# A two-layer perceiver: the state space cut into a leading part and a recurrence, and experts built in single banks with one gelu each

## The chip, the cores and the metric

The kernel runs on one core of a Trainium2 chip. The time is device microseconds of one execution. Before the change three runs gave 2102.15, 2106.83 and 2114.19 us, a median of 2106.83 us. A further execution was taken with the hardware profiler; it took 2099.58 us.

## The reference

`x` holds 64 sequences of 32 tokens with 256 features, 2048 tokens in all. Six residual steps follow each other, three per layer:

```python
x = x + _L0_xattn_ref(_layernorm(x), ctx, ctx, mask, ...)   # cross-attention
x = x + _L0_attn_ref(_layernorm(x), ...)                    # RWKV time and channel mix
x = x + _L0_ffn_ref(_layernorm(x), Wg, We, be)              # 8 experts 256->256, top 2
x = x + _L1_xattn_ref(_layernorm(x), ctx, ...)              # 16 heads, quantised linears
x = x + _L1_attn_ref(_layernorm(x), ...)                    # state space, 16 states
x = x + _L1_ffn_ref(_layernorm(x), ...)                     # 8 experts 256->512->256
```

The change touches the last two. The state space projects to 512 channels `x_main` and 512 channels `z`, runs a causal convolution of width 4 and a SiLU, and then a recurrence for each channel and each of 16 states, before it multiplies by `silu(z)`, projects back and normalises:

```python
dA = jnp.exp(A[None] * dt[:, :, None])
dBx = dt[:, :, None] * B_t[:, None, :] * x_t[:, :, None]
h = dA * h + dBx
y = jnp.einsum('bdn,bn->bd', h, C_t) + D * x_t
```

The last step computes all eight experts for every token, adds them up and scales the sum by a gate near one:

```python
h = jax.nn.gelu(jnp.einsum('nd,edh->neh', xf, w1) + b1, approximate=False)
y = jnp.einsum('neh,ehd->ned', h, w2) + b2
out = (y * norm_g[:, None, None]).sum(axis=1)
```

## The kernel before

The 2048 tokens are cut into four blocks of 512 (`NBLK`, `BT`), each four tiles of 128 tokens; `x` stays in on-chip memory all through. Each residual step is a stage, and each stage a function that is called once per block: `s0` and `s1` (attention and RWKV of the first layer), `s2` (top-2 experts, matmuls at L625), `s3` (second attention, 16 small tiles per block in `tile3`: scores at L811, exponentials at L813), `s4` (state space, `_stage4`) and `s5` (eight experts, `_stage5`). All matmuls that the change touches are in f32.

*What sets the order.* `layers` emits the stages block by block. The emission order gives each instruction its rank; from it a scheduler makes one fixed order for each engine when the kernel is built, and each engine works its own queue in that order. So an instruction that waits holds up all that stands behind it on its engine. Buffers come from pools: a `tag` with `bufs=n` has n buffers that are used in turn, and a new tile waits until the last reader of the tile that held its buffer is done. The accumulation memory is shared in the second half of the kernel by the bank (128x512 f32): two for `k.ps` (attention), two for `k.psh` (all of the state space, one bank a tile), two for `k.psu` (one tile of two banks: all of `s5` apart from its sums) and two for `k.psacc` (the sums of the experts).

*Emission around the change* (end of `layers`): `s2(1)`, `s3(1)`, `s4(0)`, `s2(2)`, `s2(3)`, and then for b = 1, 2, 3: `s3(b+1)` while there is one, `s4(b)`, `s5(b-1)`; at the end `s5(3)`. Below, "attention b", "recurrence b" and "experts b" are these stages for block b.

*State space, one block.* Statistics and norm, transposes, `project(0..3)` (L929), convolution on DVE, SiLU on ACT, a projection to the rows of B and C (L951), which go to DRAM, and to dt (L959), whose softplus is built of several ACT and DVE steps. GpSimd (POOL) forms `dtx` (L975). Then comes the recurrence: for each of 16 states a load that spreads a row of B and one of C over all partitions (`bc`), and for each pair of channel groups: `g = dtx*B` on POOL (L987, 128x1024), and for each of the two groups an exponential on ACT (L991), a scan on DVE (L992) and a product with C on DVE (L993); then POOL adds `hc` to `y` (L994). Sixteen sequences of 32 lie in one scan of 512; a large dt at each first token makes the decay there vanish. After the last state: `z` (`project(4..7)`), its SiLU and product, the residual's norm, the out-projection (L1004, L1005), and a layer norm whose last steps are on POOL.

*Experts, one block.* Norm and transposes, the gate (L1074 to L1100), and then 16 steps `h` over pairs of hidden chunks of 128. `up(h)` fills two banks: for each chunk one bf16 matmul of three rows, which adds the bias as the sum of three bf16 pieces (L1116), and two f32 matmuls with `w1` (L1118); one gelu of 128x1024 moves both to `hid` (L1120). `down(h)` adds four matmuls with `w2` (L1127) to the sums. `up(h+2)` is emitted ahead of `down(h)`. Then the sums are transposed back, scaled, added to `x` and stored tile by tile (L1144).

Of the kernel before, what the change touches and what calls it, by code (L numbers as in the profile page):

```python
# [8 lines left out]
F32 = mybir.dt.float32  # L9
# [6 lines left out]
P = 128  # L16
# [860 lines left out]
def _stage4(k, w, wk):  # L877

    nc, i = k.nc, k.i
# [29 lines left out]

    def tmp(shape, name):
        return wk.tile(shape, F32, name=name, tag="t4", bufs=3)

    def block(b):
        xs = [k.x[b][:, j, :] for j in range(4)]
        mv, rstd = _stats(k, xs, "4")
        xn = []
        for j in range(4):
            t = wk.tile([P, D], F32, name="xn4", tag="xn4", bufs=4)  # L920
            _norm(k, t, xs[j], mv, rstd, j)
            xn.append(t)
        xT = wk.tile([P, 2, BT], F32, name="xT4", tag="xT4")
        _to_channels(k, xn, lambda c, ps: nc.scalar.copy(xT[:, c, :], ps), ph)

        def project(o):
            ps = ph([P, BT], "inps")
            for c in range(2):
                nc.tensor.matmul(ps, win[:, c, o * P : (o + 1) * P], xT[:, c, :], start=c == 0, stop=c == 1)  # L929
            return ps  # L930

        xc = wk.tile([P, C, 16, T], F32, name="xc", tag="xc", bufs=1)
        for c in range(C):
            xpad = xpads[c % 2]
            nc.scalar.activation(
                xpad[:, :, 3:], project(c).rearrange("p (b t) -> p b t", t=T), AF.Identity, bias=_chan(k, "L1_attn_in_proj_b", c)
            )
            nc.vector.tensor_scalar(
                xc[:, c], xpad[:, :, 0:T], _chan(k, "conv_w0", c), _chan(k, "L1_attn_conv_b", c), ALU.mult, ALU.add
            )  # L940
            for j in range(1, 4):
                nc.vector.scalar_tensor_tensor(
                    xc[:, c], xpad[:, :, j : j + T], _chan(k, f"conv_w{j}", c), xc[:, c], ALU.mult, ALU.add
                )
        nc.scalar.activation(xc, xc, AF.Silu)
        xcf = xc.rearrange("p c b t -> p c (b t)")


        ssm_ps = ph([2 * N, BT], "ssm_ps")
        for c in range(C):  # L950
            nc.tensor.matmul(ssm_ps, wx[:, c, 0 : 2 * N], xcf[:, c, :], start=c == 0, stop=c == C - 1)  # L951
        ssm = tmp([2 * N, BT], "ssm")
        nc.scalar.activation(ssm, ssm_ps, AF.Identity, bias=bx)
        rows = k.dram.tile([2 * N, BT], F32, name="rows", tag="rows", bufs=2)
        nc.sync.dma_start(rows, ssm)

        dt_ps = ph([P, BT], "dt_ps")
        for c in range(C):
            nc.tensor.matmul(dt_ps, wdt[:, c, :], xcf[:, c, :], start=c == 0, stop=c == C - 1)  # L959


        dt = wk.tile([P, BT], F32, name="dt", tag="dt")
# [10 lines left out]
        nc.vector.scalar_tensor_tensor(dt, dt, 0.0, l_, ALU.max, ALU.add)  # L973
        dtx = wk.tile([P, C, BT], F32, name="dtx", tag="dtx", bufs=1)
        nc.gpsimd.tensor_tensor(dtx, xcf, dt.unsqueeze(1).to_broadcast([P, C, BT]), ALU.mult)  # L975

        nc.gpsimd.memset(dt.rearrange("p (b t) -> p b t", t=T)[:, :, 0:1], 1e20)
        y = xcf
        for c in range(C):
            nc.scalar.activation(y[:, c, :], y[:, c, :], AF.Copy, scale=_chan(k, "L1_attn_D", c))  # L980
        bc_rows = rows.rearrange("(two n) t -> n two t", two=2)
        for n in range(N):
            bc = wk.tile([P, 2, BT], F32, name="bc", tag="bc", bufs=2)
            nc.sync.dma_start(bc, bc_rows[n].partition_broadcast(P))
            for c2 in range(0, C, 2):
                g = wk.tile([P, 2, BT], F32, name="g", tag="g", bufs=3)
                nc.gpsimd.tensor_tensor(g, dtx[:, c2 : c2 + 2], bc[:, 0:1, :].to_broadcast([P, 2, BT]), ALU.mult)  # L987
                hc = wk.tile([P, 2, BT], F32, name="hc", tag="hc", bufs=2)
                for c in range(2):
                    h = ph([P, BT], "h")  # L990
                    nc.scalar.activation(h, dt, AF.Exp, scale=A[:, c2 + c, n : n + 1])  # L991
                    nc.vector.tensor_tensor_scan(h, h, g[:, c, :], 0.0, ALU.mult, ALU.add)  # L992
                    nc.vector.tensor_tensor(hc[:, c, :], h, bc[:, 1, :], ALU.mult)  # L993
                nc.gpsimd.tensor_tensor(y[:, c2 : c2 + 2], y[:, c2 : c2 + 2], hc, ALU.add)  # L994

        for c in range(C):
            zs = tmp([P, BT], "zs")
            nc.scalar.activation(zs, project(C + c), AF.Silu, bias=_chan(k, "L1_attn_in_proj_b", C + c))
            nc.gpsimd.tensor_tensor(y[:, c], y[:, c], zs, ALU.mult)
        for j in range(4):  # L1000
            _norm(k, xn[j], xs[j], mv, rstd, j)
# [12 lines left out]
    return block  # L1014
# [5 lines left out]
def _stage5(k, w, tmp, out):  # L1020
# [17 lines left out]

    at = CHAN_AT["L1_ffn_b1"]
    left = tmp.tile([P, E * H], F32, name="left", tag="left")  # L1040
    nc.vector.tensor_copy(left, k.chan[:, at : at + E * H])
    b1d = k.dram.tile([3, E * H, P], BF16, name="b1d", tag="b1d")
    for q in range(3):
        piece = tmp.tile([P, E * H], BF16, name="piece", tag=f"piece{q}")
        nc.vector.tensor_copy(piece, left)
        nc.vector.tensor_tensor(left, left, piece, ALU.subtract)
        pc_ps = k.ps.tile([E * H, P], BF16, name="pc_ps", tag="s")
        nc.tensor.transpose(pc_ps, piece, k.identb)
        rows = tmp.tile([E * H, P], BF16, name="pc_rows", tag=f"pc_rows{q}")
        nc.scalar.copy(rows, pc_ps)  # L1050
        nc.scalar.dma_start(b1d[q], rows)
    one3 = w.tile([3, 1], BF16, name="one3", tag="one3")
    nc.gpsimd.memset(one3, 1.0)
# [6 lines left out]
    def block(b):  # L1060
        xs = [k.x[b][:, j, :] for j in range(4)]
        mv, rstd = _stats(k, xs, "5")
        xn = []
        for j in range(4):
            t = k.wk5.tile([P, D], F32, name="xn5", tag="xn5", bufs=4)
            _norm(k, t, xs[j], mv, rstd, j)
            xn.append(t)
        xT = k.wk5.tile([P, 2, BT], F32, name="xT5", tag="xT5", bufs=1)
        _to_channels(k, xn, lambda c, ps: nc.scalar.copy(xT[:, c, :], ps), ps)
# [33 lines left out]
        w1, w2, b1 = {}, {}, {}  # L1103

        def up(h):
            e, q = divmod(h, H)
            if q == 0:
                w1[e] = k.wk5.tile([P, 2, H * P], F32, name="w1", tag="w1")
                w2[e] = k.wk5.tile([P, H, D], F32, name="w2", tag="w2")
                b1[e] = k.wk5.tile([3, H, P], BF16, name="b1e", tag="b1e")  # L1110
                nc.sync.dma_start(w1[e], w1d[e])
                nc.sync.dma_start(w2[e], w2d[e])
                nc.sync.dma_start(b1[e], b1d[:, H * e : H * e + H, :])
            u = ps([P, 2, BT], "up")
            for f in range(2):
                nc.tensor.matmul(u[:, f, :], b1[e][:, q + f, :], one3.to_broadcast([3, BT]), start=True, stop=False)  # L1116
                for c in range(2):
                    nc.tensor.matmul(u[:, f, :], w1[e][:, c, (q + f) * P : (q + f + 1) * P], xT[:, c, :], start=False, stop=c == 1)  # L1118
            t = k.wk5.tile([P, 2, BT], F32, name="hid", tag="hid")
            nc.scalar.activation(t, u, AF.Gelu)  # L1120
            return t

        def down(h, t):
            e, q = divmod(h, H)
            for f in range(2):
                for o in range(2):
                    nc.tensor.matmul(  # L1127
                        acc[o], w2[e][:, q + f, o * P : (o + 1) * P], t[:, f, :], start=h + f == 0, stop=h + f == E * H - 1
                    )

        t = up(0)
        for h in range(0, E * H, 2):
            later = up(h + 2) if h + 2 < E * H else None
            down(h, t)
            t = later
        res = k.wk5.tile([P, 2, BT], F32, name="res", tag="hid")
        for o in range(2):
            nc.scalar.activation(res[:, o, :], acc[o], AF.Identity, bias=b2s[:, o : o + 1])
        for j in range(4):
            rT = ps([P, D], "rT")  # L1140
            for o in range(2):
                nc.tensor.transpose(rT[:, o * P : (o + 1) * P], res[:, o, j * P : (j + 1) * P], k.ident)  # L1142
            t = k.wk5.tile([P, D], F32, name="o5", tag="xn5", bufs=4)
            nc.vector.scalar_tensor_tensor(t, rT, gt[:, j : j + 1], xs[j], ALU.mult, ALU.add)  # L1144
            nc.sync.dma_start(out[(4 * b + j) * P : (4 * b + j + 1) * P, :], t)
# [4 lines left out]
def layers(k, out):  # L1150
# [32 lines left out]
    with right, left:  # L1183
        pool = opened(left, "left")
        k.psh, k.psu, w4 = pool("psh", 2, **psum), pool("psu", 1, **psum), pool("w4", 1)
        s4 = _stage4(k, w4, pool("wk4", 2))
        with right2:
            s2(1)
            s3(1)
            s4(0)  # L1190
            s2(2)
            s2(3)
        k.psacc, w5 = pool("psacc", 2, **psum), pool("w5", 1)
        with ExitStack() as es:
            s5 = _stage5(k, w5, opened(es, "right")("tmp5", 1), out)
        k.wk5 = pool("wk5", 2)
        for b in range(1, NBLK):
            if b + 1 < NBLK:
                s3(b + 1)
            s4(b)  # L1200
            s5(b - 1)
# [82 lines left out]
```

## Time and profile before

| | |
|---|---|
| median of three runs | 2106.83 us (2102.15 to 2114.19) |
| profiled execution | 2099.58 us |
| its span | 2097.8 us |
| mean granted TensorE clock | 0.838 of full speed |
| instructions | 20886 |
| ACT table loads at the gelu's line / at the exponential's L991 | 47 / 33, 1283 ns each |

The span is the time between the first and the last instruction in the trace. In a group's row, the columns are line, engine, operation, output and inputs, shape and count, then busy us and mean ns of one, then idle us of the engine just before these instructions and what ended most of that idle time. The engines are PE (matmul), PEld (weight load, beside PE), DVE, ACT, POOL and SP (which only issues loads and stores here). One f32 matmul with 512 columns leaves two matmul records in the trace. The 40 slices of the page show the granted clock in tenths; it swings between half and full within the span:

```profile
PE   4778967668989878885879999979999859873798
...
PEclk8677977878989977555887999978999969986799
```

Stages by first and last instruction of their lines in the trace, in us from the span's start:

| stage | from | to |
|---|---|---|
| attention 1 | 755 | 1017 |
| recurrence 0 (POOL, L975 to L994) | 799 | 998 |
| attention 2, with experts 0 | 1110 | 1410 |
| recurrence 1 | 1126 | 1323 |
| attention 3, with experts 1 | 1411 | 1700 |
| recurrence 2 | 1469 | 1645 |
| recurrence 3, with experts 2 | 1752 | 1912 |
| out-projection of block 3 (PE) | 1912 | 1933 |
| experts 3 (PE) | 1950 | 2095 |

### The profile page before, as it was taken

Reading aid. Unit: us, or ns where it says so; the run is one execution under the profiler, and the core shown is the slowest. Engines: PE = TensorE matmul, PEld = TensorE weight load, DVE = VectorE, ACT = ScalarE, POOL = GpSimd, SP = SyncE. Lnnn points to the kernel's source line nnn. Section 1 sums busy time; section 2 is a strip of 40 time slices with the busy share of each in tenths; the row PEclk is TensorE's granted clock in tenths of the full one; section 3 lists DMA queues with packets and bytes.
Section 4 is the critical chain, followed back from the end, with each engine's and each line's share of the span. In section 5 each row is a group of like instructions: output and inputs, shape, how many; then the busy total and the mean of one; then the engine's idle time right before and its main releaser. Section 6 shows DMA issues by size and latency. Waiting matters only on the chain. (4 is left out here: it accounts for less than half of the span.)

```text
span 2097.8 us, 20886 instructions
## 1 busy us (share of the span) xinstructions
PE 1711.6 (82%) x6778; PEld 831.9 (40%) x6778; DVE 1349.9 (64%) x2559; ACT 920.8 (44%) x1932; POOL 1009.7 (48%) x1078
## 2 busy tenths in 40 slices
PE   4778967668989878885879999979999859873798
PEld 2334534334545433442434444434444423322333
DVE  4588493765584567999666888545888663775100
ACT  3445342302434235554115677526777527652111
POOL 4445445312121315888414788430888545996100
PEclk8677977878989977555887999978999969986799
DMA  7654232210000101232002333111233103340011
GB/s 236 222 182 148 92 116 80 72 41 0 21 21 21 58 7 55 61 71 61 0 0 68 105 107 105 31 33 49 71 113 108 41 0 91 101 121 21 30 60 40
DMA packets 88007, 150.10 MB, mean 72 GB/s; under 512 B 8040, under 2 KB 52442, under 8 KB 85850
## 3 DMA queue, kind: packets, MB, share of 16 engines
q1 hardware_dynamic: 85188, 147.79, 23.0%
q10 hardware_dynamic: 2710, 0.98, 0.2%
q8 instruction: 53, 0.87, 0.2%
q14 instruction: 56, 0.46, 0.1%
HBM read 137.81 MB, written 10.94 MB: 71 GB/s over the span
## 5 line engine op out<-in xcount | busy, mean ns | idle before, releaser
L992 DVE TENSOR_TENSOR_SCAN h<-h,g 128x512 f32<-128x512 f32 x256 | 305.9, 1218 | 57.9 <-ACT h L991 45.3
L987 POOL TENSOR_TENSOR g<-dtx,bc 128x1024 f32<-128x1024 f32 x128 | 299.1, 2352 | 73.5 <-DMA bc<-rows 51.6
L994 POOL TENSOR_TENSOR xc<-xc,hc 128x1024 f32<-128x1024 f32 x128 | 300.0, 2351 | 48.0 <-DVE hc L993 32.3
L1118 PE MATMUL up<-xT,w 128*128 128x512 f32 x512 | 279.0, 654 | 0.0
L1127 PE MATMUL acc<-hid,w 128*128 128x512 f32 x512 | 246.6, 611 | 0.8 <-ACT hid L1120 0.8
L991 ACT ACTIVATE h<-dt,A 128x512 f32<-128x512 f32 x256 | 173.5, 688 | 121.7 <-DVE hc L993 120.4
L811 PE MATMUL sc<-kT,qm 32*128 32x257 f32 x512 | 177.5, 498 | 16.0 <-ACT p L813 10.9
L993 DVE TENSOR_TENSOR hc<-h,bc 128x512 f32<-128x512 f32 x256 | 171.0, 679 | 8.8 <-POOL xc L994 4.9
L813 ACT ACTIVATE p<-sc,nm 128x257 f32<-128x257 f32 x256 | 119.6, 470 | 107.9 <-DVE nm L812 106.8
L812 DVE TENSOR_REDUCE nm<-sc 128x1 f32<-128x257 f32 x256 | 102.6, 416 | 90.8 <-PE sc L811 89.7
L625 PE MATMUL weps<-we,xT 128*128 128x512 f32 x256 | 137.2, 677 | 27.2 <-DVE x L627 26.1
L89 POOL TENSOR_TENSOR rs_t<-rs_r 128x4 f32<-128x4 f32 (+3 forms) x150 | 32.8, 220 | 239.6 <-DVE rs_r L87 204.3
L1127 PEld LDWEIGHTS acc<-hid,w 128*128 128x128 f32 x512 | 93.4, 193 | 104.4 <-issue 102.5
L811 PEld LDWEIGHTS sc<-kT,qm 32*128 32x128 f32 x512 | 79.2, 213 | 125.5 <-ACT p L813 51.3
L1118 PEld LDWEIGHTS up<-xT,w 128*128 128x128 f32 x512 | 87.0, 198 | 94.6 <-issue 93.5
L1120 ACT ACTIVATE hid<-up 128x1024 f32<-128x1024 f32 x64 | 65.5, 1023 | 104.5 <-PE up L1118 103.9
L230 POOL TENSOR_TENSOR cT<-cT,scb 128x2056 f32<-128x2056 f32 x16 | 74.6, 4662 | 52.5 <-DMA scb<-scales 43.0
L929 PE MATMUL inps<-xT,w_L_attn_in_projT 128*128 128x512 f32 x128 | 72.8, 704 | 31.3 <-DVE hc L993 31.3
L525 POOL TENSOR_TENSOR kk<-kk 128x512 f32<-128x512 f32 x32 | 33.2, 1040 | 119.4 <-ACT kk L524 119.4
L1144 DVE SCALAR_TENSOR_TENSOR o<-rT,gt,x 128x256 f32<-128x256 f32 x16 | 7.6, 476 | 128.6 <-PE rT L1142 128.4
L824 PE MATMUL pt_ps<-ident,p 128*128 128x128 f32 x512 | 86.4, 312 | 2.1 <-DVE kT L789 0.8
L625 PEld LDWEIGHTS weps<-we,xT 128*128 128x128 f32 x256 | 50.9, 213 | 88.6 <-issue 59.8
(391 smaller groups left out, 3210.3 us busy)
## 6 DMA issues: line engine op xcount, KB each, us to landing
bc<-rows SPq DMA_DIRECT2D x64, 512.0 KB
w<-in_L_ffn_w_dram SPq DMA_DIRECT2D x64, 512.0 KB
cT<-in_ctxT_dram SPq DMA_DIRECT2D x16, 1028.0 KB
cq<-cq SPq DMA_DIRECT2D x32, 514.0 KB
cn<-in_ctx_dram SPq DMA_DIRECT2D x64, 256.0 KB
scb<-scales SPq DMA_DIRECT2D x16, 514.0 KB
kb<-steps SPq DMA_DIRECT2D x16, 514.0 KB
x<-in_x_dram SPq DMA_DIRECT2D x4, 512.0 KB
```

Source lines behind the costliest of these rows:

```text
L625: nc.tensor.matmul(ps, xT[:, c, r], we[:, c, e : e + 2, :], start=c == 0, stop=c == 1)
L811: nc.tensor.matmul(sc, qm[r, e].rearrange("p l n g -> p (l n g)"), kT[r, :], start=True, stop=True)
L812: nc.vector.tensor_reduce(nm[:, h : h + 1], sc, AX.X, ALU.max, negate=True)
L813: nc.scalar.activation(p[:, h, :], sc, AF.Exp, bias=nm[:, h : h + 1], accum_out=sm[:, e, h : h + 1])
L824: nc.tensor.transpose(pt_ps[:, h, :], p[:, h, m * P : (m + 1) * P], k.ident)
L987: nc.gpsimd.tensor_tensor(g, dtx[:, c2 : c2 + 2], bc[:, 0:1, :].to_broadcast([P, 2, BT]), ALU.mult)
L991: nc.scalar.activation(h, dt, AF.Exp, scale=A[:, c2 + c, n : n + 1])
L992: nc.vector.tensor_tensor_scan(h, h, g[:, c, :], 0.0, ALU.mult, ALU.add)
L993: nc.vector.tensor_tensor(hc[:, c, :], h, bc[:, 1, :], ALU.mult)
L994: nc.gpsimd.tensor_tensor(y[:, c2 : c2 + 2], y[:, c2 : c2 + 2], hc, ALU.add)
L1118: nc.tensor.matmul(u[:, f, :], w1[e][:, c, (q + f) * P : (q + f + 1) * P], xT[:, c, :], start=False, stop=c == 1)
L1127: nc.tensor.matmul(acc[o], w2[e][:, q + f, o * P : (o + 1) * P], t[:, f, :], start=h + f == 0, stop=h + f == E * H - 1)
```

## The change

The state space is cut in two functions. `ahead(b)` holds everything up to dt, with an accumulation bank of its own (`psp`); `recur(b, v)` holds the rest. `xc` gets two buffers, `g` two for three; the SiLU of z is built in pairs in the buffers of `g`, and the residual's norm is built again in a buffer of `hc`. `layers` emits `ahead` of the next block in front of the recurrence of the present one, `s2(2)` in front of both. `psu` becomes one bank.

In the experts the bias matmuls and their three bf16 pieces go. Each hidden chunk is built in the one bank of `psu` and moved to `hid` with its bias added, by DVE for even chunks and by ACT for odd ones; after four chunks one gelu works in place over 128x2048. The down-projection of an expert runs one expert behind the up-projection. With the sums in `psacc`, three banks are in use. `xn5` and the output tile share one buffer of two tiles (four buffers of one before), `res` takes the buffer of `xT5`, and a block's output leaves in two stores.

```diff
-    def block(b):
+    def ahead(b):
+        v = Ctx()
...
-        xc = wk.tile([P, C, 16, T], F32, name="xc", tag="xc", bufs=1)
+        xc = wk.tile([P, C, 16, T], F32, name="xc", tag="xc")
...
+        return v
+
+    def recur(b, v):
+        xs = [k.x[b][:, j, :] for j in range(4)]
+        dt, y = v.dt, v.y
...
-                g = wk.tile([P, 2, BT], F32, name="g", tag="g", bufs=3)
+                g = wk.tile([P, 2, BT], F32, name="g", tag="g", bufs=2)
...
-        for c in range(C):
-            zs = tmp([P, BT], "zs")
-            nc.scalar.activation(zs, project(C + c), AF.Silu, bias=_chan(k, "L1_attn_in_proj_b", C + c))
-            nc.gpsimd.tensor_tensor(y[:, c], y[:, c], zs, ALU.mult)
-        for j in range(4):
-            _norm(k, xn[j], xs[j], mv, rstd, j)
+        for c2 in range(0, C, 2):
+            zs = wk.tile([P, 2, BT], F32, name="zs", tag="g", bufs=2)
+            for f in range(2):
+                nc.scalar.activation(
+                    zs[:, f, :], project(v, C + c2 + f, ph), AF.Silu, bias=_chan(k, "L1_attn_in_proj_b", C + c2 + f)
+                )
+            nc.gpsimd.tensor_tensor(y[:, c2 : c2 + 2], y[:, c2 : c2 + 2], zs, ALU.mult)
+        xn = wk.tile([P, 4, D], F32, name="xe4", tag="hc", bufs=2)
...
+        for n in range(E * H + H):
+            e, q = divmod(n, H)
+            if e < E:
...
+                    hid[e] = k.wk5.tile([P, H, BT], F32, name="hid", tag="hid")
+                u = ps([P, BT], "up")
                 for c in range(2):
-                    nc.tensor.matmul(u[:, f, :], w1[e][:, c, (q + f) * P : (q + f + 1) * P], xT[:, c, :], start=False, stop=c == 1)
-            t = k.wk5.tile([P, 2, BT], F32, name="hid", tag="hid")
-            nc.scalar.activation(t, u, AF.Gelu)
-            return t
...
+                    nc.tensor.matmul(u, w1[e][:, c, q * P : (q + 1) * P], xT[:, c, :], start=c == 0, stop=c == 1)
+                b1 = _chan(k, "L1_ffn_b1", n)
+                if q % 2:
+                    nc.scalar.activation(hid[e][:, q, :], u, AF.Identity, bias=b1)
+                else:
+                    nc.vector.tensor_scalar(hid[e][:, q, :], u, b1, None, ALU.add)
+                if q == H - 1:
+                    nc.scalar.activation(hid[e], hid[e], AF.Gelu)
+            e -= 1
+            if e >= 0:
                 for o in range(2):
                     nc.tensor.matmul(
-                        acc[o], w2[e][:, q + f, o * P : (o + 1) * P], t[:, f, :], start=h + f == 0, stop=h + f == E * H - 1
+                        acc[o], w2[e][:, q, o * P : (o + 1) * P], hid[e][:, q, :], start=n == H, stop=n == E * H + H - 1
                     )
...
-        s4 = _stage4(k, w4, pool("wk4", 2))
+        ahead, recur = _stage4(k, w4, pool("wk4", 2))
         with right2:
             s2(1)
+            v = ahead(0)
             s3(1)
-            s4(0)
             s2(2)
+            later = ahead(1)
+            recur(0, v)
             s2(3)
...
         for b in range(1, NBLK):
+            v = later
             if b + 1 < NBLK:
                 s3(b + 1)
-            s4(b)
+                later = ahead(b + 1)
+            recur(b, v)
             s5(b - 1)
         s5(NBLK - 1)
```

## The prediction

> **What bounds the kernel now.** I read the page's table of engines first, then the windows of busy time cut at the borders of the stages (found by the lines' first and last instructions), then the chain that ended last. No engine is full over the span:
>
> ```profile
> span 2097.8 us, 20886 instructions
> ...
> PE 1711.6 (82%) x6778; PEld 831.9 (40%) x6778; DVE 1349.9 (64%) x2559; ACT 920.8 (44%) x1932; POOL 1009.7 (48%) x1078
> ```
>
> The windows (start:end, length; busy us of PE, weight loads, DVE, ACT, POOL with counts; granted PE clock; DMA share; GB/s):
>
> ```profile
> 799.00:998.00 199.00, 147.62 (x637) 77.60 (x638) 180.90 (x280) 96.98 (x235) 159.31 (x80) 0.54 0.21 56
> 998.00:1126.00 128.00, 108.31 (x321) 52.42 (x320) 79.11 (x223) 26.84 (x46) 32.14 (x101) 0.86 0.07 22
> 1126.00:1323.00 197.00, 185.61 (x805) 80.92 (x804) 168.76 (x249) 138.34 (x255) 155.38 (x78) 0.95 0.32 89
> ...
> 1469.00:1645.00 176.00, 172.19 (x774) 76.80 (x773) 149.86 (x228) 128.78 (x237) 147.90 (x64) 0.98 0.32 96
> ...
> 1752.00:1912.00 160.00, 113.03 (x256) 43.11 (x254) 115.02 (x131) 95.76 (x111) 149.16 (x65) 0.88 0.35 99
> ...
> 1950.00:2097.00 147.00, 139.56 (x328) 57.65 (x328) 5.47 (x22) 21.71 (x23) 2.36 (x12) 0.94 0.15 47
> ```
>
> Row 1 is recurrence 0 beside attention 1: DVE is 91% busy and sets the end. Row 2 is the stretch between two recurrences (top-2 experts of blocks 2 and 3, block 1's projection). Rows 3 and 4 are recurrences 1 and 2 beside attention 2 and 3 and, interleaved, the experts of blocks 0 and 1: PE is 94% and 98% busy, so the experts fill PE while DVE and POOL do the recurrence. Row 5 is recurrence 3 with the experts of block 2 under it: POOL 93%. Row 6 is block 3's experts alone. The chain has that tail in a fixed beat of 7.89 us for two hidden chunks:
>
> ```profile
> 2000.39 1.91 PE up L1118 x4
> 2002.62 1.91 PE up L1118 x4
> 2004.53 3.43 PE acc L1127 x8
> 2008.28 1.91 PE up L1118 x4
> ```
>
> The 2000.39 to 2008.28 beat holds 2 x 1.91 + 3.43 = 7.25 us and, as the rest, two bias matmuls and gaps (0.64). So the end is the sum of three attention stages, the gaps between recurrences, recurrence 3 at POOL's pace, and PE alone in the tail.
>
> **The change, part by part.** Baseline is the profiled execution, 2099.58 us: span 2097.8 and 1.8 around it. The median of the three runs, 2106.83, lies 7.25 above it. Where work goes I read from the fixed order of the changed kernel's instructions on each engine; a PE row of the trace is half a matmul there, because these matmuls leave two records each.
>
> *Leading part (statistics, in-projection, convolution, softplus) ahead of another block's recurrence, with its own bank.* Work is the same; its matmuls, evictions, convolution and one store of B and C rows move on PE, ACT, DVE and SP. In SP's order the store of block 1's rows stands behind all sixteen row loads of recurrence 0 and ahead of those of recurrence 1, so nothing queues behind it that could run earlier: 0. Gain: row 2 ends earlier. The top-2 experts of block 2 now mix with the start of attention 1, so between recurrences 0 and 1 only block 3's experts and a projection are left, about 63 us after attention 1's end at 1012; attention 2 and recurrence 1 start at about 1075, against 1110 and 1126: -35 and -51. Later "ahead" parts still wait for their attention stage, which gives their input, and are followed by the recurrence at once: the 51 to 58 us from attention's end to the product dt*x (52 for block 3, 1700 to 1752) stay. So the overlap is real only for blocks 0 and 1.
>
> *Banks.* The leading part's own bank is taken from the experts: they build each up-projection in one bank where it was two side by side; the recurrence keeps two. What that costs is in the experts' terms and in rival C. *g in two buffers instead of three.* POOL makes g, DVE scans and multiplies (0.68 each), POOL adds (2.35). Bounds: 0 where POOL sets the pace (64 x 2.35 = 150 of recurrence 3's 160), and up to 1 us per pair (32 us a recurrence) where DVE must finish two scans before the next g begins. The scan's group says how near g is to being the last to come:
>
> ```profile
> L992 DVE TENSOR_TENSOR_SCAN h<-h,g 128x512 f32<-128x512 f32 x256 | 305.9, 1218 | 57.9 <-ACT h L991 45.3 <-POOL g L987 5.3 <-POOL xc L994 3.5
> L987 POOL TENSOR_TENSOR g<-dtx,bc 128x1024 f32<-128x1024 f32 x128 | 299.1, 2352 | 73.5 <-DMA bc<-rows 51.6 <-DVE h L992 11.6 <-DVE kT L789 2.8
> ```
>
> Of 57.9 us of idle before all 256 scans ACT's exponential ends 45.3 and g only 5.3, so g is mostly there with time to spare; but a scan that has to free a buffer already holds POOL up for 11.6 in all four. I take 5 us a recurrence at most and 0 in the sum.
>
> *Experts.* 128 bias matmul records of 396 ns go (50.7 us of PE, about 12.7 a block). The 64 gelus of 1023 ns become 32 of twice the width, and 128 plain evictions with bias are added, half on DVE, half on ACT: nearest row is the 128x512 ACT exponential, 688 ns, and the DVE product from the same banks, 679 ns. That is 16 x 0.68 = 11 us per block on each. In the tail the beat becomes 7.25; 16 beats save 10, but the first expert has no down-projection to hide its four evictions (about 4 x 0.9), and the last gelu (2.05) and four down steps stand alone: about 123 us against 130.
>
> *A rule against the row, ACT.* The Trainium skill, "ScalarE: Activation LUTs", section "What ACT_TABLE_LOAD costs", puts a load at about 1283 ns and some 1.4 more for the drain. The trace has the 1283 too, 47 loads at the gelu's line and 33 at the exponential's, 102.6 us. By the rule, one gelu per expert would take half the switches and give back some 100 us of ACT. By the rows it gives nothing: ACT is 44% busy, 60% in row 5, and the tail uses one table. I take 0.
>
> *What the order moves, and this decides.* Before, experts 0 ran inside recurrence 1 and experts 1 inside recurrence 2. In the changed order, half of each expert's evictions stand in DVE's queue, spaced one per some eight instructions of a recurrence, and the experts' first norms stand behind recurrence 1's last scans. On PE, 548 matmuls of attention 2 run in one piece without an expert between them; the 156 matmuls of experts 0 come after it, with block 2's projection, ahead of most of attention 3; experts 1 share PE with attention 3's last 340 matmuls, where no recurrence runs; 92 of experts 2's come beside recurrence 3, and 61 are left behind its output projection. Then experts 3's norms wait for experts 2's last output store, since they share one buffer that was four.
>
> Sum: attention 2 beside recurrence 1, as row 1 but with no experts, takes about what attention 1 took (755 to 1017, 262 us): I take 258, to 1333 (before 1410). *Second rule against a row.* "TensorE: Matmul & The Clock Gate", "The HAM clock gate": PE that has no idle gap above some 3.4 us runs at the full clock. Row 1 has PE busy 148 of 199 us and a clock of 0.54. By the rule the clock would be 1.00 as in busier stretches and only DVE's 121 (recurrence) and about 100 (attention) would bound it: 226 us. I take the row's. Then 58 to recurrence 2 at 1391 (before 1469). Experts 0 hold PE to about 1485 (156 matmuls of 0.9 us with the projection). Attention 3 from there: 211 matmuls x 0.33 = 70, output projection 12, the remaining 340 with 62 of the experts about 150: end 1716, against 1700. Recurrence 3 at 1768, +16, for 160 us; its output projection ends at 1949 (before 1933). After that: layer norm wait 9, of which half is hidden, 53 matmuls of experts 2 x 0.9 = 48, their transposes, store and experts 3's norms 24, experts 3 123, end 10: about 207, against 165. Span 2097.8 + 16 + 42 = 2156; 2158 with what lies around it; on the median's footing 2165.
>
> **Rivals.**
> *A (0.66), above: slower*, because experts 0 leave recurrence 1 and a part of experts 2 comes out behind recurrence 3. Range 2130 to 2200.
> *B (0.13): faster.* Attention 3 packs. For it: rows 3 and 4 show PE can be 94 to 98% busy with experts beside attention, and 51 us fewer of bias. It decides if attention 3 ends before 1647: recurrence 3 then ends 70 sooner, and even with 207 behind it the median is 2095 or less; at 1640, 2089. Against it: 300 us of PE work (attention 3, experts 0, part of experts 1) would have to fit into 1391 to 1640.
> *C (0.14): much slower.* Lockstep: an expert's next up-projection waits for its single bank, whose eviction waits in DVE's queue behind scans that wait for g. At 1 us for each of 32 pairs in two recurrences, +60: 2225. Against it: POOL's pace already is 2.35 us per instruction.
> *D (0.07): no change.* The 77 us won by 1333 pay all of what experts 0 push back, and the tail's 42 are met by what is left of it: 2107.
>
> **How the numbers follow.** Likeliest A, 2165. A measurement of this kernel tells about 0.5% from no change, so 2096 to 2117 is "same". Faster is B, 0.13; same is D, 0.07; slower is A and C, 0.80. The range leaves out less than half of B and half of C: 2094 to 2222. A alone: 2130 to 2200.
>
> **What would show it.** Right: attention 2 beside recurrence 1 at a granted clock near 0.5 and DVE near 90%; experts 0's first up-projection after about 1275; recurrence 3's first g at 1750 to 1790; about 48 us of up and down matmuls of block 2 after recurrence 3's last output projection; experts 3's beat 7.25. Wrong: recurrence 3 starting before 1690 (B), a recurrence longer than 190 us with POOL under 80% (C), or the tail behind recurrence 3's output projection at 165 or less.

## The result and the profile after

The changed kernel took 2181.73 us (median of four runs, 2178.64 to 2184.82) against 2110.51 us for the kernel before on the same footing: a ratio of 1.034, 95% interval 1.029 to 1.038. The profiled execution took 2181.74 us, with a span of 2180.0 us. In one of the runs below (two banks shared by the leading part and the experts) two of 20 executions took 3073 and 3669 us, and its ratio leaves them out.

The page of the changed kernel, in its table of engines and four of its groups (columns as before):

```profile
PE 1770.9 (81%) x6647; PEld 881.3 (40%) x6647; DVE 1398.3 (64%) x2616; ACT 894.9 (41%) x1907; POOL 1009.5 (46%) x1069
...
L997 POOL TENSOR_TENSOR g<-dtx,bc 128x1024 f32<-128x1024 f32 x128 | 300.6, 2353 | 108.2 <-DVE h L1002 43.1
...
L1116 PE MATMUL up<-xT,w 128*128 128x512 f32 x512 | 278.4, 660 | 67.9 <-DVE hid L1121 52.1
L1004 POOL TENSOR_TENSOR xc<-xc,hc 128x1024 f32<-128x1024 f32 x128 | 300.9, 2352 | 22.9 <-DVE hc L1003 22.7
...
L811 PE MATMUL sc<-kT,qm 32*128 32x257 f32 x512 | 216.6, 579 | 15.2 <-ACT p L813 13.3
```

The last group before the change:

```profile
L811 PE MATMUL sc<-kT,qm 32*128 32x257 f32 x512 | 177.5, 498 | 16.0 <-ACT p L813 10.9
```

The bias matmuls, 50.7 us of PE, are gone, and yet PE is busy for 59 us longer. The score matmuls of the attention (L811) have not changed, but one takes 579 ns where it took 498: more of the attention runs at half the clock. An eviction is the instruction that moves a finished tile from its bank to on-chip memory. One wait is new, PE's 52.1 us for DVE's evictions, and one has grown: POOL waits 43.1 us for scans before g, where it waited 11.6.

The windows of the changed kernel, cut at its own stages:

```profile
1086.00:1292.00 206.00, 170.75 (x752) 92.19 (x751) 181.70 (x294) 108.75 (x258) 161.25 (x83) 0.55 0.23 65
...
1390.00:1586.00 196.00, 170.85 (x552) 79.68 (x552) 154.76 (x221) 115.74 (x202) 158.50 (x71) 0.76 0.29 81
1586.00:1728.00 142.00, 135.12 (x640) 66.79 (x640) 59.82 (x166) 61.09 (x139) 24.71 (x71) 0.95 0.12 38
...
1780.00:1958.00 178.00, 119.22 (x238) 49.83 (x237) 141.88 (x167) 83.26 (x106) 153.99 (x81) 0.78 0.30 80
...
1978.00:2042.00 64.00, 49.83 (x117) 21.48 (x116) 12.13 (x31) 12.51 (x12) 10.52 (x32) 0.94 0.21 66
```

Row 1 is recurrence 1 beside attention 2: it had experts inside and a clock of 0.95, and now has none and 0.55. Row 2 is recurrence 2, with experts 0 in its first half. Row 3 is what is left of attention 3, with experts 1: PE is 95% busy, and DVE and POOL, freed of the recurrence, stand at 42% and 17%. Row 4 is all but the ends of recurrence 3, which now takes 180 us. Row 5 is new: the rest of experts 2 with nothing to hide under. The chain through it, start and length in us:

```profile
2023.10 1.92 ACT hid L1123
2025.06 7.15 PE acc L1127 x16
2034.87 2.15 DMA out_dram<-o
2038.70 2.14 DMA out_dram<-o
2051.38 3.79 PE up L1116 x4
```

Block 2's experts end and are stored before block 3's first up-projection starts at 2051.38.

Stage by stage, with the prediction's value between the two traces (us; recurrences by `dtx` and the last sum into `y`; by this measure recurrence 2 before the change ends at 1655, not 1645, and takes 186 us, and recurrence 3 ends at 1916, not 1912):

| | before | predicted | after |
|---|---|---|---|
| recurrence 1 starts | 1126 | 1075 | 1086 |
| attention 2 starts | 1110 | 1075 | 1083 |
| attention 2 ends | 1410 | 1333 | 1343 |
| recurrence 2 starts | 1469 | 1391 | 1390 |
| experts 0 leave PE | 1378 | 1485 | 1487 |
| attention 3 ends | 1700 | 1716 | 1728 |
| recurrence 3 starts | 1752 | 1768 | 1775 |
| recurrence 3 takes | 164 | 160 | 180 |
| out-projection of block 3 ends | 1933 | 1949 | 1977 |
| from there to the end | 165 | 207 | 203 |

### The profile page after: what moved, and what is told of

Same layout as the page of the kernel before. It is cut to its first block, busy times and chain, and to the rows that moved or that the text cites. A ratio compares the mean times of both kernels' runs of the same rounds, so it can differ in the third digit from the quotient of the medians.

```text
span 2180.0 us, 20697 instructions
## 1 busy us (share of the span) xinstructions
PE 1770.9 (81%) x6647; PEld 881.3 (40%) x6647; DVE 1398.3 (64%) x2616; ACT 894.9 (41%) x1907; POOL 1009.5 (46%) x1069
## 5 line engine op out<-in xcount | busy, mean ns | idle before, releaser
L997 POOL TENSOR_TENSOR g<-dtx,bc 128x1024 f32<-128x1024 f32 x128 | 300.6, 2353 | 108.2 <-DVE h L1002 43.1
L1116 PE MATMUL up<-xT,w 128*128 128x512 f32 x512 | 278.4, 660 | 67.9 <-DVE hid L1121 52.1
L1127 PE MATMUL acc<-hid,w 128*128 128x512 f32 x512 | 255.0, 624 | 10.8 <-ACT hid L1123 10.8
L811 PE MATMUL sc<-kT,qm 32*128 32x257 f32 x512 | 216.6, 579 | 15.2 <-ACT p L813 13.3
L1116 PEld LDWEIGHTS up<-xT,w 128*128 128x128 f32 x512 | 97.6, 204 | 204.0 <-issue 93.0
L1127 PEld LDWEIGHTS acc<-hid,w 128*128 128x128 f32 x512 | 100.4, 201 | 136.8 <-issue 116.8
L1121 DVE TENSOR_SCALAR hid<-up,chan 128x512 f32<-128x512 f32 x64 | 47.7, 745 | 158.2 <-PE up L1116 158.1
L811 PEld LDWEIGHTS sc<-kT,qm 32*128 32x128 f32 x512 | 97.2, 249 | 128.2 <-ACT p L813 70.8
L625 PE MATMUL weps<-we,xT 128*128 128x512 f32 x256 | 135.0, 657 | 7.0 <-DVE x L627 6.0
L1119 ACT ACTIVATE hid<-up,chan 128x512 f32<-128x512 f32 x64 | 43.8, 684 | 200.7 <-PE up L1116 200.3
L824 PE MATMUL pt_ps<-ident,p 128*128 128x128 f32 x512 | 100.1, 354 | 5.2 <-ACT pl L818 3.1
L824 PEld LDWEIGHTS pt_ps<-ident,p 128*128 128x128 f32 x512 | 82.3, 184 | 23.5 <-DVE kT L789 9.1
```

The costliest lines, as they stand in the source:

```text
L625: nc.tensor.matmul(ps, xT[:, c, r], we[:, c, e : e + 2, :], start=c == 0, stop=c == 1)
L811: nc.tensor.matmul(sc, qm[r, e].rearrange("p l n g -> p (l n g)"), kT[r, :], start=True, stop=True)
L824: nc.tensor.transpose(pt_ps[:, h, :], p[:, h, m * P : (m + 1) * P], k.ident)
L1116: nc.tensor.matmul(u, w1[e][:, c, q * P : (q + 1) * P], xT[:, c, :], start=c == 0, stop=c == 1)
L1127: nc.tensor.matmul(acc[o], w2[e][:, q, o * P : (o + 1) * P], hid[e][:, q, :], start=n == H, stop=n == E * H + H - 1)
```

## The experiments

My theory was that the experts leave the recurrences because with one bank and the last rank they find no place in the order beside the scans. The rivals were the single bank as a price at every chunk, the two g buffers, and the split itself. Each run has its own ratio to the kernel before, with its interval. The kernel before took 2103 to 2111 us beside the different runs, so where times of different runs are set against each other, a few us say nothing, and the ratios are the better guide.

**Experts emitted first.** In the changed kernel:

```diff
-            recur(b, v)
             s5(b - 1)
+            recur(b, v)
```

> The changed kernel with one line moved: the experts of block b-1 are emitted ahead of recurrence b instead of behind it, so that they have the higher rank; banks, buffers, evictions and gelus are those of the change. Theory (the experts are pushed out of the recurrences because, with the lower rank, their evictions stand behind the recurrence's scans in DVE's order): experts 0 run beside attention 2 and recurrence 1 again, nothing of experts 2 is left behind block 3's out-projection, and the early gain of some 35 to 50 us stays: 2060 to 2100 us. Rival 1 (one bank for the up-projection costs PE a wait at each chunk, wherever the experts stand): 2140 us or more. Rival 2 (two g buffers stretch the recurrences): 2150 us or more, recurrence 3 still at 178 us. If the experts' evictions delay the scans as much as they gain, recurrences 1 and 2 grow to 230 us and the time is near 2140.

Measured: 2111.41 us, ratio 1.003 (1.001 to 1.004). Moving one line brings the loss from 3.4% to 0.3%, so it gives back some nine tenths of it. The two recurrences in its windows:

```profile
1092.00:1312.00 220.00, 206.30 (x838) 95.31 (x838) 182.59 (x292) 129.73 (x253) 158.20 (x91) 0.88 0.30 87
...
1457.00:1661.00 204.00, 187.49 (x831) 84.86 (x830) 174.44 (x266) 130.27 (x259) 153.05 (x66) 0.93 0.34 91
```

PE is 94% and 92% busy again, at a clock of 0.88 and 0.93, and block 2's experts leave PE at 1889, inside recurrence 3, which takes 160 us. Experts 0's first norms, on DVE, run at 1107 instead of 1281. The first two rivals fall as main causes. But the time is above the band of my theory, 2060 to 2100: recurrence 1 starts 35 us earlier than before the change, recurrence 2 only 11 earlier, recurrence 3 25 later. Recurrences 1 and 2 last 220 and 204 us, against 197 and 186 before.

**The new experts alone, with one bank.** In the kernel before, `_stage5` is that of the change, and `psu` is one bank; the rest stays, three g buffers too.

> The kernel before with the new experts alone (one bank for the up-projection, plain evictions on DVE and ACT, one gelu for each expert); the state space stays in one part with three g buffers and the old emission. Theory (experts displaced by their evictions' rank): as slow as the changed kernel or slower, since the early gain of the moved top-2 experts is missing: 2180 to 2240 us, experts 0 starting behind recurrence 1. Rival 2 (g buffers) and rival 3 (the split of the state space and its emission push the experts out): no slower than before, 2085 to 2115 us.

Measured: 2252.54 us, ratio 1.069 (1.066 to 1.072). The loss is there without the split, and larger, above my band of 2180 to 2240. Its windows over recurrence 1 and the stretch behind it:

```profile
1140.00:1340.00 200.00, 159.63 (x707) 86.38 (x706) 175.99 (x282) 102.69 (x248) 155.20 (x78) 0.53 0.22 58
1340.00:1481.00 141.00, 129.11 (x325) 59.98 (x324) 39.32 (x113) 33.97 (x43) 32.37 (x89) 0.95 0.18 56
```

It is the same picture, so the split falls as the main cause too: attention 2 at half clock with the recurrence, then 141 us of experts 0 with POOL at 23%. Here the experts do begin inside the recurrence, and stop. Their third chunk, on PE and then in DVE's eviction:

```profile
1161.31 2.08 PE L1101 MATMUL up<-xT,w 128*128 128x512 f32 x2
```

```profile
1336.66 0.68 DVE L993 TENSOR_TENSOR hc<-h,bc 128x512 f32<-128x512 f32 x1
...
1337.43 0.74 DVE L1106 TENSOR_SCALAR hid<-up,chan 128x512 f32<-128x512 f32 x1
```

The chunk is built at 1163 and waits 174 us for its eviction, which stands in DVE's fixed order behind the recurrence's last products. With one bank PE can build no other chunk meanwhile. The leading part of block 2 comes behind them, so that recurrence 2 starts at 1533.

**The new experts alone, with two banks in turn.** As above, with one number changed:

```diff
-pool("psu", 1, **psum)
+pool("psu", 2, **psum)
```

> As the run with the new experts alone, but with two banks in turn for the up-projection, as much accumulation memory as before the change. Theory (rank and queue): with a second bank PE can build a chunk while one waits for its eviction, the experts stay mostly beside the recurrences; gain of the bias matmuls some 10 us in the tail: 2080 to 2120 us. Rival 1 (plain evictions and their waits themselves): 2150 us or more.

Measured: 2136.76 us, ratio 1.013 (1.009 to 1.018), a little above the band. The second bank is worth 116 us at the last rank, with the state space in one part: experts 0 run from 1130 to 1423, from attention 2's start. So a better rank helps beside the split and a second bank helps without it; the change had neither. A second bank at the last rank, in the changed kernel and not shared with the recurrence, was not run.

**The top-2 experts moved, alone.** In the kernel before:

```diff
-            s4(0)
             s2(2)
+            s4(0)
```

> The kernel before with one line moved: the top-2 experts of block 2 are emitted ahead of block 0's state space instead of behind it, nothing else. My step for the early gain puts recurrence 1 some 40 to 50 us earlier by this alone; with everything behind it as before the change: 2055 to 2075 us. If the time between recurrences 0 and 1 is set by something else (the split, the own bank), 2095 to 2115 us.

Measured: 2108.86 us, ratio 1.001 (1.000 to 1.003). That is the second case of the expectation: this move alone brings nothing. Recurrence 0 starts at 865 instead of 799, recurrence 1 at 1143 instead of 1126. The top-2 experts go ahead only at recurrence 0's cost, unless block 0's leading part goes ahead of both, as in the change.

**The bank given back to the experts.** In the changed kernel the leading part builds in `psh`, which it then shares with the recurrence, and `psu` has two banks:

```diff
-        k.psh, k.psp, k.psu = pool("psh", 2, **psum), pool("psp", 1, **psum), pool("psu", 1, **psum)
+        k.psh, k.psu = pool("psh", 2, **psum), pool("psu", 2, **psum)
```

> The changed kernel with one bank moved: the leading part has none of its own and builds in the recurrence's two, the experts' up-projection gets two in turn; emission, evictions, gelus and two g buffers as in the change. Theory now (the experts leave the recurrences because with one bank each chunk must wait for an eviction that has the last rank on DVE; the two runs on the kernel before put 116 us on the second bank): experts 0 beside attention 2 again, 2095 to 2140 us. If the own bank is what gives the leading part its early start, recurrence 1 begins at 1120 or later and the time is 2140 to 2160. If the rank alone decides (as the run with experts emitted first could be read), 2170 us or more.

Measured: 2360.14 us, ratio 1.120 (1.113 to 1.126). None of the three expectations had this. Recurrence 0 in its window, cut at 1029, and its scans (count, shortest/median/longest ns, first and last start):

```profile
791.00:1029.00 238.00, 191.94 (x964) 98.11 (x962) 126.84 (x336) 78.91 (x225) 28.63 (x78) 0.78 0.08 27
1029.00:1190.00 161.00, 81.38 (x329) 41.55 (x329) 143.31 (x195) 80.11 (x165) 149.33 (x65) 0.53 0.25 64
```

```profile
L1002 DVE TENSOR_TENSOR_SCAN h<-h,g x64: 1208/1222/1232, 1030.5 to 1185.5; 128x512 f32<-128x512 f32 x64
```

Recurrence 0 takes 399 us where it took 203. POOL makes its product and two g from 791 on, and then the first scan comes only at 1030: the leading part of block 1 is emitted ahead of the recurrence, so its tiles have the earlier turns in the shared banks, and it can only run when attention 1 is done (its last matmuls, for dt, start at 1029 to 1032). From there the recurrence takes 161 us, at POOL's pace. So the leading part must not share banks with the recurrence; that it needs a bank of its own is not shown, and a run below has it share with the experts.

**Three g buffers.** In the changed kernel (the table `b2` goes into a buffer of the attention, for room):

```diff
-g = wk.tile([P, 2, BT], F32, name="g", tag="g", bufs=2)
+g = wk.tile([P, 2, BT], F32, name="g", tag="g", bufs=3)
```

> The changed kernel with three g buffers as before the change (a small bias table of the experts is laid into a buffer of the attention to make room), nothing else. My prediction put 0 on the third buffer; the profile of the changed kernel has POOL waiting 43.1 us for scans before g where 11.6 stood before. Theory that this wait is on the path only where POOL sets the pace: recurrence 3 goes from 180 to about 165, the others by less, 2155 to 2172 us. Lockstep theory (each recurrence 15 us shorter, the experts' pace with it): 2110 to 2140. If POOL's wait is hidden: 2175 to 2190.

Measured: 2187.38 us, ratio 1.038 (1.031 to 1.044): the same as the change. Its two POOL groups, to be held against those of the page above:

```profile
L997 POOL TENSOR_TENSOR g<-dtx,bc 128x1024 f32<-128x1024 f32 x128 | 299.2, 2352 | 78.1 <-DMA bc<-rows 56.5
L1004 POOL TENSOR_TENSOR xc<-xc,hc 128x1024 f32<-128x1024 f32 x128 | 300.1, 2351 | 61.4 <-DVE hc L1003 55.9
```

The idle time before g falls by 30.1 us, and that before the sum into `y` grows by 38.5. POOL waits for the same scans, one instruction later. This is the case in which POOL's wait is hidden. A wait that appears in a profile after a change is not yet a price.

**All three suspects undone.** Bank given back as above, experts emitted first, three g buffers.

> The changed kernel with the bank given back to the experts, the experts emitted ahead of the recurrence, and three g buffers: all three suspects undone, the split, its early emission, the plain evictions and the one gelu kept. If they are the whole loss and the split's early start of 35 to 50 us is real, 2050 to 2090 us, faster than before the change. If the evictions with bias themselves cost what the bias matmuls did (DVE and ACT beside attention), 2095 to 2120.

Measured: 2356.17 us, ratio 1.119 (1.113 to 1.124). That is outside both bands. Recurrence 0 takes 412 us. It repeats the lesson of the shared banks and says nothing of the rest.

**The split with the old experts.** `_stage5` of before, the leading part in the recurrence's banks.

> The other half of the change alone: the state space split and emitted early, two g buffers, but the leading part builds in the recurrence's banks and the experts are those of before (two banks, bias matmuls, a gelu for each pair of chunks straight from the bank). If the split gives what it gives beside the new experts (2252.5 without it, 2181.7 with it): 2035 to 2070 us. If its early start is paid back by the experts' leftover behind block 3's out-projection, as in the moved top-2 experts: 2085 to 2115 us.

Measured: 2397.45 us, ratio 1.138 (1.132 to 1.144), outside both bands for the same reason (412 us for recurrence 0). This arrangement could not show the split's own gain. Two other runs bear on it: beside the same new experts in one bank the kernel takes 2252.5 us without the split and its emission, and 2181.7 with them, some 70 us less.

**Two banks shared by the leading part and the experts.** In the changed kernel `psp` goes, `psu` gets two banks, the leading part builds there, and the emission is:

```diff
             if b + 1 < NBLK:
                 s3(b + 1)
-                later = ahead(b + 1)
-            recur(b, v)
             s5(b - 1)
+            if b + 1 < NBLK:
+                later = ahead(b + 1)
+            recur(b, v)
```

> The changed kernel with two banks shared in turn by the leading part and the experts' up-projection (the same eight banks in all), and emission attention b+1, experts b-1, leading part b+1, recurrence b, so that the leading part's turn comes behind the experts', never ahead of the recurrence's. Theory (two causes: the recurrence must not share banks with the leading part, which the three runs at 2356 to 2397 us with recurrences of 400 us suggest; and the experts need rank or a second bank to stay beside the recurrence): about the run with the experts emitted first (2111) less the waits of PE for DVE's evictions there (some 28 + 39 us, part of it hidden): 2075 to 2105 us. If evictions on DVE and ACT are what pays back the early start, 2105 to 2125. If a leading part behind the experts in the banks' turn loses its early start, 2125 or more.

Measured: 2101.24 us, ratio 0.998 (0.997 to 1.000), inside the theory's band and some 3.5% better than the change. It differs from the change in three things at once: the experts' place in the order, the leading part's place behind them, and two banks in turn that both use. It is level with the kernel before, not faster. Recurrences 1 and 2:

```profile
1093.00:1316.00 223.00, 210.84 (x887) 97.19 (x886) 189.31 (x304) 135.93 (x260) 159.63 (x92) 0.92 0.32 90
1440.00:1645.00 205.00, 197.98 (x860) 88.74 (x860) 173.28 (x281) 135.36 (x261) 156.04 (x79) 0.95 0.32 92
```

PE is 95% and 97% busy, POOL 72% and 76%, and recurrence 1 holds more of PE's records than before the change (887 against 805). So I take PE to set the length of these stages, which would leave an early start to move work rather than to save it; no run tests this by itself.

**The same with the old experts**, one tile of two banks at a time, which the leading part takes as well.

> As the run before it, but with the experts of before the change (bias matmuls, two banks side by side, gelu straight from them, one tile of two banks at a time, shared with the leading part). If the split's early start of 35 to 50 us survives without the new evictions, and these are what paid it back: 2055 to 2085 us. If attention beside experts and recurrence runs no faster for either form: 2095 to 2115 us.

Measured: 2167.89 us, ratio 1.030 (1.026 to 1.034), outside both bands. It is 67 us above the run before it, so nothing here says that the new form of the experts paid the early start back. Two things differ, the form and the number of tiles in turn, and this run doesn't part them. Recurrences 1 and 2 are as long as there (218 and 208 us).

**All evictions on ACT.** In the changed kernel:

```diff
-                if q % 2:
-                    nc.scalar.activation(hid[e][:, q, :], u, AF.Identity, bias=b1)
-                else:
-                    nc.vector.tensor_scalar(hid[e][:, q, :], u, b1, None, ALU.add)
+                nc.scalar.activation(hid[e][:, q, :], u, AF.Identity, bias=b1)
```

> The changed kernel with all the experts' plain evictions on ACT, none on DVE. If it is DVE's queue that holds the experts up (as the prediction said: evictions behind scans), PE's 52 us of waits for DVE evictions go and experts 0 and the rest behind block 3's out-projection shrink: 2140 to 2165 us. If it is the single bank, whichever engine empties it: 2170 to 2200 us, since ACT then takes 16 more evictions per block beside exponentials.

Measured: 2148.03 us, ratio 1.021 (1.017 to 1.025), 27 us below the change by the ratios and 34 by the medians. The time is in the band that I had given to DVE's queue, but experts 0 have not moved: they still start at 1312, and recurrence 3 at 1774.6 instead of 1775.0. That does not clear DVE's queue. In the changed kernel DVE has, at the end of recurrence 1:

```profile
1274.63 1.28 DVE L1003 TENSOR_TENSOR hc<-h,bc 128x512 f32<-128x512 f32 x2
...
1280.94 1.13 DVE L115 TENSOR_SCALAR xn<-x,mv,rstd 128x256 f32<-128x256 f32 x2
```

The second row is the experts' first norms. They stand on DVE behind the recurrence's last products, and in this run they do so too, at 1281.41. So no chunk was waiting for its bank or its eviction before that, and this run shows only that the evictions on DVE are not what holds experts 0 up.

The gain comes late: in the two traces recurrence 3 takes 169 us instead of 180, and the stretch from there to the end of the kernel is 22 us shorter. The chain of the changed kernel has this within recurrence 3:

```profile
1892.34 0.69 DVE hc L1003
1893.04 0.67 DVE hid L1121
1893.75 1.27 PE up L1116 x2
1895.02 3.27 PE acc L1127 x4
1898.29 0.87 PE up L1116 x2
1899.18 0.69 ACT hid L1119
1901.62 1.22 DVE h L1002
```

An even chunk's eviction stands behind a product on DVE. PE must have it before it can build the odd chunk, and that one's eviction stands on ACT with the recurrence's exponentials behind it, for which the next scan waits. In recurrence 3 ACT's evictions wait 25.2 us for PE this way in the changed kernel, and 5.0 with all evictions on ACT. But that is not shown to be what made the recurrence longer. In the run with the new experts alone and one bank, evictions alternate too, and ACT waits in recurrence 3 (engine and line, waited for, us in total, times, longest):

```profile
ACT hid L1104 <- PE up L1101: 28.5, 9, 5.6
```

There recurrence 3 takes 165 us, with all of experts 2's down-projection under it. And with all evictions on ACT, DVE has less to do as well, which this run doesn't part from the alternation.

**Two buffers for the norm and output tiles.** In the changed kernel `xn5` and `o5` get `bufs=2`.

> The changed kernel with two buffers for the experts' norm and output tiles instead of one, nothing else. The prediction has 24 us between experts 2's last matmul and experts 3's first, from the shared buffer that waits for the output stores: by that step 2160 to 2172 us. If that time is the gate's chain and not the buffer: 2176 to 2188 us.

Measured: 2158.88 us, ratio 1.028 (1.023 to 1.033); a hair under the band that I had given to the buffer, but the interval meets the change's. From block 2's last down-projection to block 3's first up-projection it is 15.4 us (2027.4 to 2042.8) where the change has 19.2 (2032.2 to 2051.4). So in these traces the shared buffer is worth some 4 us there; the rest I take to be the chain of norm, transposes and gate. The profiled execution was the slowest of the four (2174.85), and what made the others faster it can't show.

## Why the prediction was right, step by step

**The displacement** was right in kind and size. Experts 0 leave PE within 2 us of the forecast, and the run with the experts emitted first shows that their place in the order is nearly the whole loss. The reason was the one that the traces show: the first norms stand on DVE behind recurrence 1's last products, and where the norms come earlier, with the new experts alone, an eviction does. What I left out is that the number of banks decides how much gets past such an eviction: a second one was worth 116 us there.

**Recurrence 2's start**, within 1 us, is luck. Attention 2 ended 10 us later than forecast, and from there it took 47 us to the recurrence instead of 58.

**"-35 and -51" for the early start** were too large, -27 and -40, and the reason was incomplete. Block 2's top-2 experts do mix into attention 1, as I said: their matmuls (L625) run from 764 to 836 instead of 790 to 1047. But moved alone they only hold up recurrence 0. It takes block 0's leading part ahead of them, in banks apart from the recurrence's.

**Recurrence 3, "for 160 us"**, is the term that was mis-sized most: 180. In the profiled executions the span is 2180, and my sum 2156. Of these 24 us, 7 are recurrence 3's later start, 20 its length and 1 its out-projection, and the tail gives 4 back. On the medians it is 2182 against 2165. Rival C's reason, a lockstep through the single bank, would fit a longer recurrence, but C put it at 60 us in two recurrences, and recurrences 1 and 2 are not longer than before (192 and 179 us, against 197 and 186). For recurrence 3 putting all evictions on ACT takes 11 us away; why it is longer stays open, since the same alternation left it at 165 in another run.

**The tail** was right, 203 against 207, and so were its parts: what is left of experts 2 takes 55 us (52 or 53 in the sum), the turnaround 19 (24), experts 3 119 (123), the end 10. The parts as written add up to 209.5 and not 207. Of the turnaround the buffer is some 4 us.

**"0 in the sum" for g** was right; three buffers change nothing.

**The clock** followed the row and not the rule of the Trainium skill, "TensorE: Matmul & The Clock Gate", "The HAM clock gate": attention 2 beside recurrence 1 ran at 0.55. The changed kernel's clock, cut where it falls, and PE's wait just before that:

```profile
1086.00:1099.00 13.00, 8.80 (x31) 3.95 (x30) 9.03 (x20) 4.72 (x8) 11.60 (x5) 1.00 0.24 81
1099.00:1283.00 184.00, 152.95 (x676) 83.54 (x673) 169.86 (x267) 96.69 (x238) 144.89 (x65) 0.50 0.22 61
```

```profile
1098.33 1.03 PE L774 MATMUL vl_ps<-vr,pick 4*4 4x128 f32 x8 [3.96 <-ACT vr L771]
```

The fall comes right behind an idle stretch of 3.96 us, above the rule's 3.4. But then the clock is at half for 184 us in which PE never waits longer than 2.7 us. Before the change, in row 1, it fell at 822 and was at half for 171 us; in the 70 us ahead of that no idle stretch was longer than 2.4 us (row 1 has one of 18.5 us, but only from 970 on). So the rule alone does not give these stretches, and what holds the clock down stays open; the matmuls' ends are modelled.

**The gelus.** ACT's table loads at the gelu's and the exponential's line fell from 80 to 31 (20 and 11), 63 us of ACT. The sum put it at 0. No run takes it by itself, so what it is worth is not shown.

**The rivals.** B, faster, needed attention 3 to end before 1647; it ended at 1728, since PE was 95% busy from 1586 on. D was right in its first half only: 79 us were won by recurrence 2's start, and all of them were spent by recurrence 3's.

What stays open is whether the split can be a gain with the experts in place. The early start is real (33 to 36 us at recurrence 1 in the three runs that have the split and the experts inside), but those recurrences take 18 to 25 us longer than before the change. The experts' higher rank ahead of the recurrence is common to them. A bank of its own for the leading part, together with two for the experts, would take nine banks and wasn't tried.

## What to carry to other kernels

When filler work shares a kernel with a slow chain, look at what lets the filler in: its rank and how many tiles it can have under way. Taking away one of its two banks cost 116 us here, with the same instructions; in the changed kernel, moving one line of emission, without the bank, gave back some nine tenths of the loss. To see what stops the filler, look for its first instruction behind the chain's last one on a shared engine: here norms and evictions on DVE. Part of a stage that is moved ahead of another block must not take turns in the chain's own banks, since the chain then waits for it (399 us for 203).

## What was not expected of the hardware

PE's busy time rose by 59 us while 51 us of matmuls were taken out: with the experts gone from beside it, attention 2 ran at a granted clock of 0.55 instead of 0.95, and the attention's score matmuls of 32x257 went from 498 to 579 ns in the mean. A plain eviction of 128x512 f32 with its bias took 745 ns on DVE and 684 ns on ACT, and the gelu of 128x2048 in place 1910 ns, less than the two of 128x1024 from the banks that it replaced (2 x 1023).
